# Combining expert rows on GpSimd, one stored copy of the keys, and score maxima sent from SBUF to SBUF, in a Mamba, mixture-of-experts and latent-attention kernel

## The chip, the cores and the metric

The kernel runs on one core of one Trainium2 chip. Times are device microseconds of one execution; a stated time is the median of several runs, and the trace comes from one more execution under the hardware profiler. Five engines share the work: TensorE (PE, with PEld for its weight loads), VectorE (DVE), ScalarE (ACT), GpSimd (POOL) and SyncE (SP, which here only issues DMA transfers and reads indices into registers). POOL and ACT can issue transfers too.

## The reference

The input is x, [4, 512, 128] f32: 4 sequences of 512 tokens. Four residual steps follow one another, each over a layer norm of the whole of x:

```
x = x + A(layernorm(x))      # A: Mamba block, then mixture of experts
x = x + FFN(layernorm(x))    # hidden 384, weights dequantised from int32
x = x + ATT(layernorm(x))    # latent attention, 16 heads of 8, causal
x = x + FFN(layernorm(x))

moe: top_w, sel = top_k(softmax(h @ router_w), 2)
     out = sum over e of (sum of top_w where sel == e) * (silu(h @ Wg[e]) * (h @ Wu[e])) @ Wd[e]

att: c_kv = x @ W_dkv.T                      # 64 wide
     q_lat = (x @ W_dq.T @ W_uq.T) in heads, times k_eff
     a = softmax(causal(q_lat @ c_kv.T / sqrt(8)))
     y = a @ c_kv, per head times v_eff
```

The Mamba block has 256 inner channels, 16 states and a convolution of 4 taps; the mixture has 8 experts of width 512, and each token goes to 2 of them.

## The kernel before

The work has two parts, and the four sequences (b = 0 to 3) move through them like a pipeline.

*First part, to some 378 us.* `scan` (L901) runs 64 steps, one for each sequence and state. A step is a scan on DVE (`hst`, L916), a product on POOL (`hc`, L928), a sum over states on PE (`yp`, L873). Beside the scans four streams of small work are drained in pieces: `closing`, `tokens`, `tiles` and `ends`. When a sequence's 16 steps are done, `close(b)` (L942) makes the Mamba output, adds `base[b] = xs[b] + h2` on POOL (L971), normalises, and calls `route` and `number`, which choose the two experts of each token, their weights `gates[b]` ([128, 4, 2]: token in tile, token tile, rank) and the rows at which the token goes into a sorted array in DRAM. `scatter` (L260) sends the tokens there, `plan(g)` lists for each tile of 128 sorted rows its expert and its place (`cplan`, read by SP into registers at L352 and L353), and `experts(g)` (L333) computes the tiles. `GROUPS = [[0], [1], [2, 3]]`: sequences 0 and 1 are sorted alone, 2 and 3 together. In this part the order on PE, DVE, ACT and SP is the order in which the program is written; POOL's queue is free except that the scan's products are chained in order (`queued`, L881).

*From experts to attention.* For each sequence of a finished group, stream `tokens` runs three generators:

- `combine(b)` (L397): 8 gathers, one for each token tile t and rank k, each issued by POOL as an indirect DMA of 128 rows of 512 B (L413) into one of 8 buffers `yk`; and 8 DVE instructions (L406), `base[:, t] = yk * gate + base[:, t]`. Sequence 0 takes the rows one at a time, the others four at a time, with two turns from gather to use.
- `first_ffn(b)`: `x = base + FFN(layernorm(base))`. The layer norm's statistics are on DVE (`bn_stats` L153, `mv` L155), then `xn` on ACT (L167), transposes on PE (L176), products `pg`, `pu`, `fpd`, and the final addition on POOL (L463).
- `project(b)` (L505): the queries and keys of attention. `pu` (L524) is a matmul for each half (queries, then keys). A value is split into three bf16 parts: the first by ACT (L527), which also copies the whole (`full`, L528), the rest by POOL (L529 to L531). `parts` has one buffer. The queries' parts are stored to `q_d` in DRAM by one DMA (L533); the keys' parts are stored three times to `k_d` (L536), so that a later load finds each part repeated.

*Second part: attention.* It goes by 8 units u, two of each sequence, 8 heads each. In this part a scheduler with a model of the chip sets the order within each engine.

- `fill(u)` (L1122): SP loads two stacks of [128, 8, 512] bf16, `qs` and `ks`, three buffers of each. Rows 0 to 71 of a stack are 3 blocks of 24: each block of `qs` is all three parts of the 8 query dimensions, and block i of `ks` is part i of the keys three times. A single product over the 72 rows is so the sum of all nine products of parts. The last three rows (MXR to P) are -1 in `ks` (L1130) and the row maxima in `qs`.
- `maxima(u)` (L1138): PE makes the masked scores `sc` (L1152, L1156), DVE reduces them to maxima `mx` (L1148), splits them into three bf16 parts (`mparts`), PE transposes these (`pmx`), ACT copies them to `mT` [24, 512] (L1179), and POOL sends `mT` to `m_d` in DRAM (L1181) and from there to the last three rows of `qs` (L1182).
- `exps(G)` (L1188): PE makes the transposed scores minus maxima, `st` (L1205, L1213), ACT the exponentials `p` (L1218). `weigh(G)` sums the values on PE (`po` L1232), transposes, normalises and adds on POOL (`base = x + yn`, L1262).
- `last(b)` runs the final FFN beside later units, and stores the output.

Every tile that `tmp` (L208) makes has as many buffers as its pool, two; the plan's tiles on one partition (`cge`, `cof`, `cat`, `cplan`) are among them.

Of the kernel before, what the change touches and what calls it, by code (L numbers as in the profile page):

```python
# [8 lines left out]
F32 = mybir.dt.float32  # L9
I32 = mybir.dt.int32  # L10
BF16 = mybir.dt.bfloat16
AF = mybir.ActivationFunctionType
ALU = mybir.AluOpType
# [3 lines left out]
P = 128  # L17
B, L, C = 4, 512, 128
NT = L // P
# [6 lines left out]
NH, HS, KVL = 16, 8, 64  # L26
# [11 lines left out]
def block_kernel(ctx, tc, x, rms1_w, rms2_w, in_proj_w, conv_w, conv_b, x_proj_w,  # L38
                 dt_proj_w, dt_proj_b, A_log, D_skip, out_proj_w, router_w, Wg, Wu, Wd,
                 W_dq, W_dqT, W_uqT, W_dkvT, W_uk, W_uv, W_oT, w_gateT, w_upT, w_downT, out):  # L40
    nc = tc.nc
# [143 lines left out]
    base = [keep.tile([P, NT, C], F32, tag="base", name=f"base{b}") for b in range(B)]  # L185
    gates = [keep.tile([P, NT, 2], F32, tag="gates", name=f"gates{b}") for b in range(B)]
    hits = [keep.tile([P, NT, 2, NEXP], F32, tag="hits", name=f"hits{b}") for b in range(B)]
    rows = [keep.tile([P, NT, 2], I32, tag="rows", name=f"rows{b}") for b in range(B)]
    rows_y = [keep.tile([P, NT, 2], I32, tag="rows_y", name=f"rows_y{b}") for b in range(B)]
# [16 lines left out]


    def tmp(name, shape, dt=F32, n=P):  # L208
        return wt.tile([n] + shape, dt, tag=name, name=name)

    taken = {}

# [184 lines left out]
    def combine(b):  # L397

        g = place[b][0]

        n = 4 if b else 1
        which = [(t, k) for t in range(NT) for k in range(2)]
        got = []
        for i in range(0, len(which) + 2 * n, n):
            for yk, t, k in got[max(i - 2 * n, 0) : max(i - n, 0)]:
                nc.vector.scalar_tensor_tensor(  # L406
                    base[b][:, t, :], yk, gates[b][:, t, k : k + 1], base[b][:, t, :],
                    ALU.mult, ALU.add,
                )
            yield  # L410
            for t, k in which[i : i + n]:
                yk = wt.tile([P, C], F32, tag="yk", name="yk", bufs=8)
                nc.gpsimd.indirect_dma_start(  # L413
                    yk, None, sorted_y[g],
                    bass.IndirectOffsetOnAxis(ap=rows_y[b][:, t, k : k + 1], axis=0),
                )
                got.append((yk, t, k))
            yield


# [84 lines left out]
    def project(b):  # L505

        xn = wt.tile([P, NT, C], F32, tag="xn", name="axn", bufs=1)
        yield from layernorm(xn, xs[b])
        xT = wt.tile([P, L], F32, tag="xT", name="axT", bufs=1)
        transposed(ps, xT, xn)  # L510
        yield
        yield
        pq = ps.tile([P, L], F32, tag="mm", name="pq")
        nc.tensor.matmul(pq, w_qk[0], xT, start=True, stop=True)
        qk = wt.tile([P, L], F32, tag="qk", name="qk")
        nc.scalar.copy(qk, pq)
        yield
        q_d = dram0.tile([3, HS, NH, L], BF16, tag="q_d", name="q_d", bufs=2)
        k_d = dram0.tile([3, 3, HS, NH, L], BF16, tag="k_d", name="k_d", bufs=2)
        for half in range(2):  # L520
            yield
            rows = slice(half * KVL, (half + 1) * KVL)
            pq = ps.tile([P, L], F32, tag="mm", name="pu")
            nc.tensor.matmul(pq, w_up[rows, :], qk[rows, :], start=True, stop=True)  # L524
            full = wt.tile([P, L], F32, tag="full", name="full", bufs=1)
            parts = wt.tile([P, 3, L], BF16, tag="parts", name="parts", bufs=1)
            nc.scalar.copy(parts[:, 0, :], pq)  # L527
            nc.scalar.copy(full, pq)  # L528
            nc.gpsimd.tensor_tensor(full, full, parts[:, 0, :], ALU.subtract)  # L529
            nc.gpsimd.tensor_copy(parts[:, 1, :], full)  # L530
            nc.gpsimd.tensor_tensor(parts[:, 2, :], full, parts[:, 1, :], ALU.subtract)  # L531
            if half == 0:
                nc.gpsimd.dma_start(q_d.rearrange("j d h l -> (d h) j l"), parts)  # L533
            else:
                for j in range(3):
                    nc.gpsimd.dma_start(k_d[:, j].rearrange("i d h l -> (d h) i l"), parts)  # L536
            yield
        stores[b] = q_d, k_d, qk

# [543 lines left out]
    with ExitStack() as second:  # L1083
# [18 lines left out]
        NP9, MXR = 9 * HS, P - 3  # L1102
        NU = NH // 2
# [18 lines left out]
        def fill(u):  # L1122

            b, h0 = u // 2, (u % 2) * NU
            q_d, k_d, _ = stores[b]
            if u < 3:
                for h in range(0, NU, 2):
                    for stack in (qs[u], ks[u]):
                        nc.gpsimd.memset(stack[KVL:P, h : h + 2], 0.0)
                nc.sync.dma_start(ks[u][MXR:P], below.unsqueeze(1).to_broadcast([3, NU, L]))  # L1130
            for i in range(3):
                at = slice(3 * HS * i, 3 * HS * (i + 1))
                for stack, of in ((qs[u % 3], q_d), (ks[u % 3], k_d[i])):
                    nc.sync.dma_start(
                        stack[at], of[:, :, h0 : h0 + NU, :].rearrange("j d h l -> (j d) h l")
                    )

        def maxima(u):  # L1138

# [37 lines left out]
                )  # L1177
            mT = w2.tile([3 * NU, L], BF16, tag="mT", name="mT")
            nc.scalar.copy(mT, pm)  # L1179
            m_d = dram.tile([3, NU, L], BF16, tag="m_d", name="m_d")  # L1180
            nc.gpsimd.dma_start(m_d.rearrange("i h l -> (i h) l"), mT)  # L1181
            nc.gpsimd.dma_start(q[MXR:P, :, :], m_d)  # L1182
            yield

        scale = float(HS) ** -0.5
# [208 lines left out]
```

## Time and profile before

| | |
|---|---|
| median of 6 runs | 903.63 us (896.84, 904.18, 902.8, 903.08, 904.52, 905.38) |
| the profiled execution | 909.74 us |
| its span in the trace | 908.0 us |
| its mean granted clock of TensorE | 0.898 |

The page of the profile gives for each engine the time in which it was busy. The same, cut into stretches of the span (busy us of each engine in the stretch):

| stretch, us | what runs | length | PE | DVE | ACT | POOL | DMA share |
|---|---|---|---|---|---|---|---|
| 0 to 378 | scans | 378 | 296.87 | 321.79 | 198.22 | 216.88 | 0.39 |
| 378 to 443 | experts, first projection | 65 | 53.22 | 33.70 | 23.78 | 30.84 | 0.52 |
| 443 to 640 | attention of sequences 0 and 1, experts of 2 and 3 | 197 | 163.34 | 93.96 | 69.14 | 29.17 | 0.54 |
| 640 to 732 | combine and projection of 2, attention of 1 and 2 | 92 | 59.34 | 34.49 | 35.91 | 30.15 | 0.22 |
| 732 to 908 | attention of 2 and 3 | 176 | 140.26 | 86.76 | 84.04 | 22.26 | 0.12 |

The costliest groups of POOL and DVE that lie in the changed lines or beside them, from the group list between 400 and 900 us (line, engine, operation, out<-in, partitions x elements, count | busy us, mean ns of one | idle us of the engine just before them, and what ended it):

```profile
L413 POOL DMA_INDIRECT yk<-yg,rows_y x24 | 23.2, 967 | 84.9 <-DMA yg<-ym 59.0 <-DMA wd<-in_Wd_dram 19.2 <-issue 4.9
...
L536 POOL DMA_DIRECT2D k_d<-parts x12 | 9.3, 774 | 1.2 <-POOL parts L531 1.2
...
L406 DVE SCALAR_TENSOR_TENSOR base<-yk,gates,base 128x128 f32<-128x128 f32 x24 | 8.2, 350 | 6.9 <-DMA yk<-yg,rows_y 6.5 <-issue 0.4
...
L1181 POOL DMA_DIRECT2D m_d<-mT x8 | 4.4, 554 | 63.6 <-ACT mT L1179 63.6
L1182 POOL DMA_DIRECT2D qs<-m_d x8 | 4.2, 529 | 15.2 <-DMA m_d<-mT 8.1 <-PE pg L448 5.5 <-DVE mx L1148 1.7
```

"Idle before" is time in which that engine stood and which ended when the named work did. It costs something only where the engine is one that others wait for. The releaser named is the last one by the profile.

SP's loads of the stacks at L1134 take 0.29 to 0.48 us each to issue (`qs`, median 0.36) and 0.29 to 0.94 (`ks`, median 0.36); the three loads of -1 rows at L1130, whose source is repeated three times, take 0.78 to 0.98.

### The profile page before, as it was taken

The page shows a single profiled execution, that of the slowest core. Times are in us where ns is not written, and L with a number is a line of the kernel's source. Part 1 is how long each engine was busy: PE and PEld are TensorE (multiplying, and loading weights), DVE is VectorE, ACT ScalarE, POOL GpSimd, SP SyncE. Part 2 cuts the span into 40 slices and gives each one's busy share as a digit, 9 for nine tenths or more (in the row PEclk, how much of TensorE's full clock was granted, in tenths as well). Part 3 has the DMA queues.
Part 4 walks back from the last instruction along what each step waited for, and adds up shares of the span by engine and source line. Part 5 has one row for each costly group of instructions (what it writes and reads, how often), then busy time and mean ns, then how long its engine had stood idle before and what let it go on. Part 6 is the DMA issues. An engine that isn't in the chain of part 4 may idle for free.

```text
span 908.0 us, 12207 instructions
## 1 busy us (share of the span) xinstructions
PE 713.0 (79%) x3867; PEld 428.0 (47%) x3867; DVE 570.7 (63%) x1160; ACT 411.1 (45%) x797; POOL 329.3 (36%) x262
## 2 busy tenths in 40 slices
PE   7698697589698975687766998988585698799854
PEld 4433242133276641575554677757242254455432
DVE  4799999989988997554238631336733275457311
ACT  3847556647654540142310354452155353556741
POOL 1155755874774457772213022000613103101010
PEclk9898899889899997899878899999787798799987
DMA  5157211111475644263564166763101502220000
GB/s 133 38 215 271 70 58 50 62 67 58 136 219 181 211 125 126 83 208 125 189 178 126 45 197 216 229 162 120 43 12 38 138 1 57 81 54 15 3 13 12
DMA packets 84481, 99.18 MB, mean 109 GB/s; under 512 B 10369, under 2 KB 56457, under 8 KB 83241
## 3 DMA queue, kind: packets, MB, share of 16 engines
q1 hardware_dynamic: 78881, 87.09, 32.1%
q0 software_dynamic: 4352, 10.89, 3.6%
q8 instruction: 31, 0.51, 0.2%
q10 hardware_dynamic: 1184, 0.43, 0.2%
q14 instruction: 33, 0.27, 0.1%
HBM read 76.67 MB, written 21.63 MB: 108 GB/s over the span
## 4 chain that ended last, share of the span: by engine, by line
PE 35%; DVE 30%; issue 10%; ACT 9%; DMA 7%; POOL 6%; SPq 1%; another core or an unknown queue 0%; DVEq 0%; POOLq 0%; ACTq 0%
DVE hst L916 11%; DVE bx L895 5%; PE yp L873 4%; PE po L1232 4%; DVE mx L1148 3%; PE st L1205 3%; PE mpd L390 3%; POOL hc L928 3%; PE mpg L378 3%; ACT p L1218 3%; PE pg L448 2%; PE mpu L378 2%; PE fpd L457 2%; PE sc L1152 2%; DMA wgu<-in_Wg_dram 1%
## 5 line engine op out<-in xcount | busy, mean ns | idle before, releaser
L928 POOL TENSOR_TENSOR hc<-hst,cs 128x1024 f32<-128x1024 f32 x64 | 152.4, 2382 | 114.8 <-issue 25.8
L873 PE MATMUL yp<-hc,ident 128*128 128x512 f32 x256 | 143.5, 688 | 49.2 <-POOL hc L928 47.1
L916 DVE TENSOR_TENSOR_SCAN hst<-da,bx 128x1024 f32<-128x1024 f32 x64 | 146.3, 2287 | 8.7 <-POOL hc L928 1.3
L1148 DVE TENSOR_REDUCE mx<-sc 128x1 f32<-128x384 f32 (+3 forms) x168 | 102.1, 634 | 54.7 <-PE sc L1156 53.3
L873 PEld LDWEIGHTS yp<-hc,ident 128*128 128x128 f32 x256 | 51.0, 213 | 128.2 <-POOL hc L928 88.0
L1218 ACT ACTIVATE p<-st 128x512 f32<-128x512 f32 x160 | 90.2, 598 | 45.7 <-PE st L1213 24.5
L853 ACT ACTIVATE da<-delta,A 128x512 f32<-128x512 f32 (+1 forms) x128 | 84.9, 714 | 37.1 <-DVE hst L916 30.2
L321 DVE SCALAR_TENSOR_TENSOR thm<-thm,mpg 128x512 f32<-128x512 f32 x53 | 36.1, 681 | 88.4 <-ACT thm L384 88.2
L1152 PE MATMUL sc<-ks,qs 125*128 125x128 bf16 (+3 forms) x256 | 69.2, 324 | 26.9 <-DVE mx L1148 11.2
L895 DVE TENSOR_TENSOR bx<-du,pb 128x1024 f32<-128x1024 f32 x64 | 78.3, 1223 | 4.2 <-PE pb L863 2.0
L1205 PE MATMUL st<-qs,ks 128*128 128x512 bf16 (+3 forms) x256 | 64.1, 318 | 18.4 <-DMA qs<-m_d 7.7
L378 PE MATMUL mpg<-xTm,wgu 128*128 128x128 f32 x424 | 66.2, 293 | 7.3 <-DMA wgu<-in_Wg_dram 4.6
L378 PEld LDWEIGHTS mpg<-xTm,wgu 128*128 128x128 f32 x424 | 58.4, 206 | 19.7 <-issue 8.6
L390 PE MATMUL mpd<-wd,mh 128*128 128x128 f32 x424 | 59.9, 285 | 4.3 <-ACT xTm L371 3.4
L378 PE MATMUL mpu<-xTm,wgu 128*128 128x128 f32 x424 | 60.6, 286 | 2.8 <-DVE mh L322 2.8
L413 POOL DMA_INDIRECT yk<-yg,rows_y x32 | 30.9, 966 | 87.2 <-DMA yg<-ym 59.0
L390 PEld LDWEIGHTS mpd<-wd,mh 128*128 128x128 f32 x424 | 53.0, 196 | 9.5 <-ACT xTm L371 6.6
L378 PEld LDWEIGHTS mpu<-xTm,wgu 128*128 128x128 f32 x424 | 55.9, 203 | 3.3 <-DVE mh L322 3.0
L384 ACT ACTIVATE thm<-mpg 128x512 f32<-128x512 f32 x53 | 31.6, 596 | 54.3 <-PE mpg L378 28.6
L371 ACT ACTIVATE xTm<-mpt,r2w 128x128 f32<-128x128 f32 x53 | 19.4, 365 | 65.7 <-PE mpt L369 65.6
L1156 PE MATMUL sc<-maskq,identb 128*128 128x128 bf16 (+2 forms) x176 | 46.2, 263 | 0.0
L394 ACT COPY ym<-mpd 128x128 f32<-128x128 f32 x53 | 14.1, 265 | 68.8 <-PE mpd L390 49.4
(255 smaller groups left out, 1174.0 us busy)
## 6 DMA issues: line engine op xcount, KB each, us to landing
cs<-c_d SPq DMA_DIRECT2D x64, 256.0 KB
wgu<-in_Wg_dram SPq DMA_DIRECT2D x53, 256.0 KB
wgu<-in_Wu_dram SPq DMA_DIRECT2D x53, 256.0 KB
wd<-in_Wd_dram SPq DMA_DIRECT2D x53, 256.0 KB
xg<-zero SPq DMA_DIRECT2D x8, 1024.0 KB
qs<-q_d SPq DMA_DIRECT2D x24, 192.0 KB
k_d<-parts POOLq DMA_DIRECT2D x12, 384.0 KB
ks<-k_d SPq DMA_DIRECT2D x24, 192.0 KB
```

What stands on the lines that cost most here:

```text
L378: nc.tensor.matmul(pp[:, f, :], w[:, k, f * P : (f + 1) * P], rows_in, start=True, stop=True,)
L390: nc.tensor.matmul(pd, hT[:, f, :], w[:, f, :], start=(f == 0), stop=(f == NFC - 1))
L853: nc.scalar.activation(da[:, e, e:], delta[b][:, e, e:], AF.Exp, scale=A[:, e, n : n + 1])
L873: nc.tensor.matmul(yps[b][:, e, :], ident, hc[:, e, :], start=(n == 0), stop=(n == NS - 1))
L895: nc.vector.tensor_tensor(bxs[s], du[s // NS], taps[s][1].unsqueeze(1).to_broadcast([P, NE, L]), ALU.mult)
L916: nc.vector.tensor_tensor_scan(hst.rearrange("p e l -> p (e l)"), dec.pop(s).rearrange("p e l -> p (e l)"), bxs.pop(s).rearrange("p e l -> ...
L928: done = nc.gpsimd.tensor_tensor(hc, hst, cs.unsqueeze(1).to_broadcast([P, NE, L]), ALU.mult).ins
L1148: nc.vector.tensor_reduce(*taken, AX.X, ALU.max)
L1152: nc.tensor.matmul(sc[:, c : c + w], q[0:MXR, h, t * P : w], k[0:MXR, h, 0:w], start=(h == h0), stop=False, skip_group_check=True,)
L1156: nc.tensor.matmul(sc[:, 0 : n * w].rearrange("p (h k) -> p h k", k=w)[:, :, t * P : w], identb, maskq.unsqueeze(1).to_broadcast([P, n, P] ...
L1205: nc.tensor.matmul(pt[:, c : c + L - kt * P], k[:, h0 + j, rows], q[:, h0 + j, kt * P : L], start=(c == 0), stop=False, skip_group_check=True,
L1218: ready[G] = nc.scalar.activation(p, pt, AF.Exp, scale=scale).ins
```

## The change

Five things change:

1. One-partition tiles of `tmp` get one buffer instead of two.
2. `combine` of sequences 1 to 3: a turn is a token tile, with both its rows gathered into one tile `yk` [128, 2, 128] (two buffers instead of eight of half the size). GpSimd multiplies the tile by the two weights of each token and adds the two halves to `base`, one after the other. Sequence 0 keeps its eight DVE instructions, a row at a time, with the same two buffers.
3. `parts` has two buffers.
4. The keys' parts are stored once, by one DMA like the queries'; a load of a block of `ks` reads the 8 rows of a part three times, through an outer dimension of stride 0.
5. `m_d` is gone. ACT, right behind its copy to `mT`, issues three transfers that each take 8 rows of `mT` to one row of `qs`.

```diff
     def tmp(name, shape, dt=F32, n=P):
-        return wt.tile([n] + shape, dt, tag=name, name=name)
+        return wt.tile([n] + shape, dt, tag=name, name=name, bufs=1 if n == 1 else None)
...
-        n = 4 if b else 1
-        which = [(t, k) for t in range(NT) for k in range(2)]
-        got = []
-        for i in range(0, len(which) + 2 * n, n):
-            for yk, t, k in got[max(i - 2 * n, 0) : max(i - n, 0)]:
-                nc.vector.scalar_tensor_tensor(
-                    base[b][:, t, :], yk, gates[b][:, t, k : k + 1], base[b][:, t, :],
-                    ALU.mult, ALU.add,
-                )
-            yield
-            for t, k in which[i : i + n]:
-                yk = wt.tile([P, C], F32, tag="yk", name="yk", bufs=8)
-                nc.gpsimd.indirect_dma_start(
-                    yk, None, sorted_y[g],
-                    bass.IndirectOffsetOnAxis(ap=rows_y[b][:, t, k : k + 1], axis=0),
-                )
-                got.append((yk, t, k))
-            yield
+        lots = [(t, range(2)) for t in range(NT)] if b else [
+            (t, range(k, k + 1)) for t in range(NT) for k in range(2)
+        ]
+        got = {}
+        for i in range(len(lots) + 2):
+            if i >= 2:
+                yk, t, ks_ = got.pop(i - 2)
+                to = base[b][:, t, :]
+                if b:
+                    nc.gpsimd.tensor_tensor(
+                        yk, yk, gates[b][:, t, :].unsqueeze(2).to_broadcast([P, 2, C]), ALU.mult
+                    )
+                    for k in range(2):
+                        nc.gpsimd.tensor_tensor(to, to, yk[:, k, :], ALU.add)
+                else:
+                    nc.vector.scalar_tensor_tensor(
+                        to, yk[:, 0, :], gates[b][:, t, ks_[0] : ks_[0] + 1], to, ALU.mult, ALU.add
+                    )
+            yield
+            if i < len(lots):
+                t, ks_ = lots[i]
+                yk = wt.tile([P, 2, C], F32, tag="yk", name="yk")
+                for j, k in enumerate(ks_):
+                    nc.gpsimd.indirect_dma_start(
+                        yk[:, j, :], None, sorted_y[g],
+                        bass.IndirectOffsetOnAxis(ap=rows_y[b][:, t, k : k + 1], axis=0),
+                    )
+                got[i] = yk, t, ks_
+            yield
...
-        k_d = dram0.tile([3, 3, HS, NH, L], BF16, tag="k_d", name="k_d", bufs=2)
+        k_d = dram0.tile([3, HS, NH, L], BF16, tag="k_d", name="k_d", bufs=2)
...
-            parts = wt.tile([P, 3, L], BF16, tag="parts", name="parts", bufs=1)
+            parts = wt.tile([P, 3, L], BF16, tag="parts", name="parts", bufs=2)
...
-            if half == 0:
-                nc.gpsimd.dma_start(q_d.rearrange("j d h l -> (d h) j l"), parts)
-            else:
-                for j in range(3):
-                    nc.gpsimd.dma_start(k_d[:, j].rearrange("i d h l -> (d h) i l"), parts)
+            nc.gpsimd.dma_start((q_d, k_d)[half].rearrange("j d h l -> (d h) j l"), parts)
...
-                for stack, of in ((qs[u % 3], q_d), (ks[u % 3], k_d[i])):
-                    nc.sync.dma_start(
-                        stack[at], of[:, :, h0 : h0 + NU, :].rearrange("j d h l -> (j d) h l")
-                    )
+                nc.sync.dma_start(
+                    qs[u % 3][at], q_d[:, :, h0 : h0 + NU, :].rearrange("j d h l -> (j d) h l")
+                )
+                nc.sync.dma_start(
+                    ks[u % 3][at],
+                    k_d[i, :, h0 : h0 + NU, :].unsqueeze(0).to_broadcast([3, HS, NU, L]),
+                )
...
-            m_d = dram.tile([3, NU, L], BF16, tag="m_d", name="m_d")
-            nc.gpsimd.dma_start(m_d.rearrange("i h l -> (i h) l"), mT)
-            nc.gpsimd.dma_start(q[MXR:P, :, :], m_d)
+            for i in range(3):
+                nc.scalar.dma_start(q[MXR + i : MXR + i + 1, :, :], mT[NU * i : NU * (i + 1), :])
```

Seen from the queues: POOL loses 16 issues for the maxima and 8 key stores, and gains 12 multiplications and 24 additions; DVE loses 24 instructions; ACT gains 24 issues. In the order of the changed kernel, the last two gathers of sequence 0 stand behind the sum `base` of sequence 3 (L971) on POOL, and one gather instead of three stands ahead of the last scan product.

## The prediction

> **What bounds the kernel now.** I read the busy shares first, then the costly groups and the list of waits of the second part (440 to 910 us), then stretches and single instructions where a named wait is long. The second part is where most of the changed lines run.
>
> ```profile
> PE 713.0 (79%) x3867; PEld 428.0 (47%) x3867; DVE 570.7 (63%) x1160; ACT 411.1 (45%) x797; POOL 329.3 (36%) x262
> ```
>
> PE leads with 79%, but it is not full everywhere. Stretches of 20 us (columns: stretch, length, busy us of PE, PEld, DVE, ACT, POOL with instruction counts, granted clock, DMA share, GB/s) show where it starves:
>
> ```profile
> 640.00:660.00 20.00, 8.94 (x37) 4.13 (x37) 14.04 (x47) 0.81 (x3) 14.94 (x17) 0.67 0.16 45
> 700.00:720.00 20.00, 10.93 (x28) 5.19 (x29) 5.55 (x8) 6.72 (x13) 6.30 (x8) 0.71 0.63 160
> 760.00:780.00 20.00, 13.68 (x64) 7.72 (x64) 14.76 (x43) 4.54 (x8) 11.12 (x13) 0.74 0.51 144
> ```
>
> Between 500 and 640 the same view sums to 126.9 us of PE in 140: there PE itself is the bound. The list of waits from 440 on (engine and line, what it waited for: us in total, times, longest) names what starves it:
>
> ```profile
> ACT parts L527 <- DMA q_d<-parts: 17.3, 4, 6.6
> ...
> POOL qs L1182 <- DMA m_d<-mT: 8.1, 4, 2.8
> ...
> PE st L1205 <- DMA qs<-m_d: 7.7, 2, 5.1
> ...
> PE sc L1152 <- DVE mv L155: 7.2, 1, 7.2
> ...
> DVE base L406 <- DMA yk<-yg,rows_y: 6.5, 9, 1.7
> ...
> PE sc L1152 <- DMA ks<-k_d: 5.2, 1, 5.2
> ```
>
> Each of these is touched by the change. The chain that ended last runs through the key store and the key load before the first scores:
>
> ```profile
> 457.85 5.73 DMA k_d<-parts
> ...
> 464.46 4.73 DMA ks<-k_d
> ```
>
> On POOL three spots matter: three gathers ahead of the last scan product, the projection's second half, and the row of gathers of sequence 2 with the q row's two transfers among them.
>
> ```profile
> 362.97 0.94 POOL L413 DMA_INDIRECT yk<-yg,rows_y  x1 [0.30 <-issue]
> 363.93 2.36 POOL L928 TENSOR_TENSOR hc<-hst,cs 128x1024 f32<-128x1024 f32 x1
> ...
> 452.95 1.14 POOL L529 TENSOR_TENSOR full<-full,parts 128x512 f32<-128x512 f32 x1 [4.99 <-ACT full L528]
> ...
> 456.30 2.32 POOL L536 DMA_DIRECT2D k_d<-parts  x3 [0.30 <-POOL parts L531]
> ...
> 640.80 1.04 POOL L413 DMA_INDIRECT yk<-yg,rows_y  x1 [58.97 <-DMA yg<-ym]
> ...
> 713.42 0.52 POOL L1182 DMA_DIRECT2D qs<-m_d  x1 [5.47 <-PE pg L448]
> ```
>
> **The change, part by part.** The sum is made against the profiled execution (909.7 us, span 908.0), 6 us above the median of 903.63; I subtract its result from the median.
>
> *Scans' end.* The last product waited behind three gathers, from 360.4 to 363.9, though its scan ended at 358.2; in the changed order one gather stands there. Two gathers less at 0.96 + 0.30 us: -2.5. The last two gathers of sequence 0 now come behind base(3) (L971), and their two vector instructions (0.35 us each, plus some 2.5 us from issue to landing) stand ahead of the rms of sequence 3 on DVE: bounds 0 to +2, taken +0.5. Together **-2**.
>
> *Start of attention, 443 to 490.* With two parts buffers the second half need not wait for the q store (4.94 us in the chain, 3.16 us of ACT, 4.99 us of POOL): -5.0. The key store is one issue instead of three. Three stores landed 7.3 us after 456.3, while q's single store took 4.6 (447.1 to 451.7): -2.7. The loads could start about 7.7 us earlier. Two things give back. Key loads that repeat rows have no row of their own; the nearest issue rows are plain ones at 0.36 us and one repeated three times (L1130) at 0.83, so three per unit cost 0 to +1.5 in issue, and with longer landing I bound it at 0 to +3, taken +1.5. And combine 1 moves onto POOL: 8 gathers of 1.26 (10.1 us) as before, plus four turns. POOL's product takes 1.26 us for 128x512 and 2.38 for 128x1024, so 0.14 + 2.2 ns an element: 0.70 for the weighting (128x256) and 2 x 0.42 for the additions, with gaps 1.7 a turn, 6.8 in all. Sequence 1's base was ready at 493.0, on DVE; on POOL I get about 477.8 + 10.1 + 6.8 = 494.7 less what the earlier start gives: +1.7. Sum **-4.5**. The 24 vector instructions that vanish (8.2 us busy) are not counted: DVE is idle half the time here, and its statistics of base still stand between the reductions and now wait for POOL's additions.
>
> *500 to 640.* PE can gain at most its 13.1 idle us. Here lies sequence 1's projection, with a parts wait of 2.3 (545.45). I take **-3** (0 to -6).
>
> *640 to 732.* Removed: the stall of PE's scores at 651.95 (7.2, behind DVE's statistics, themselves behind the gathers), the parts wait at 700.57 (6.6), and the q row's path: mT copied by 704.7, both transfers through DRAM, st not before 721.91 (5.1 idle). Added: combine 2. In the changed order its last turn comes after 10 gathers, 3 turns earlier: 640.8 + 12.6 + 6.8 = 660.2 against 652.6 before, so +7.6; and sequence 2's normalised rows are transposed on PE after only 2 score blocks instead of 9 or 10, so PE stands for them. Of the 18.9 removed, some 9 are lost to PE idling for xn, and most of the rest to the same delay: **-2** (bounds -12 to +6).
>
> *732 to the end.* The parts wait at 766.35 (5.2) lies in a stretch where PE idles 6.3 of 20; the q rows' detour ends for three more units: **-5** (0 to -8).
>
> *q rows from ACT.* 24 transfers leave POOL's queue (16 issues of 0.54 us, 8.6 us) and go to ACT's, three a unit. Direct issues cost 0.29 to 0.98 us elsewhere, so 7 to 24 us of ACT, behind which p (0.6 us each, what PE's next products wait for), parts and axn queue. ACT is 45% busy, so mostly hidden; one per unit at 0.36 on the path: **+3**. Behind that stands a coupling: in the changed order these issues also wait on completion semaphores which SP's loads use, and SP's loads on theirs. No row before shows it; bounds 0 and 3 us a unit (a part of the 4.7 us that a load took to land), taken 0.25: **+2**.
>
> One buffer for one-partition tiles is costed at nothing: the plan of the last group may be written only when SP has read that of the group before. In the changed order SP's last such read stands just ahead of the load that began at 417.4 (L1130), and the write behind DVE's third th, which began at 419.7: some 2 us to spare. If SP were later, DVE's fh behind the write, and PE's fpd behind that, would wait as long.
>
> Sum: -2 - 4.5 - 3 - 2 - 5 + 3 + 2 = **-11.5**, so 903.6 - 11.5 = **892 us**.
>
> A page speaks against the key loads. The row first: in a stretch of loads the DMA share is 0.74 at 164 GB/s, and in a full one 1.02 at 396.
>
> ```profile
> 70.00:77.00 7.00, 6.50 (x16) 2.43 (x15) 6.74 (x7) 6.96 (x10) 2.45 (x2) 1.00 1.02 396
> 713.00:715.00 2.00, 1.45 (x4) 0.54 (x4) 0.84 (x3) 0.60 (x1) 0.52 (x1) 1.00 0.74 164
> ```
>
> The Trainium skill, "DMA: Bandwidth & Descriptors", section "Why a DMA increments its semaphore by 16 and not by 1", says that a transfer uses the largest number of engines up to 16 that divides the slowest dimension, other than one, of both sides. For 24 rows on both sides that is 12 of 16 or 0.75, as the row shows; for 3 repeats of 8 rows it would be 3, which no run here shows yet. An estimate from page and rows: 3/16 of 396 is some 74 GB/s, so 196.6 KB would take 2.7 us instead of 1.2, +4.5 us a unit; if all eight were exposed the sum would be +23 and not -11.5.
>
> **The rivals.** *B, all waits pay.* The list above that is removed sums to 17.3 + 7.2 + 7.7 + 5.2 = 37.4, with the scans' end 39; if combine hides behind PE's experts, two thirds arrive: -26, **878**. For it: PE's idle stretches coincide with them. Against: 500 to 640, where PE is full, and the 7.6 us by which combine 2 is later.
>
> *C, nothing comes of it.* If the projections were hidden anyway (the -3 and -5 vanish) and combine 2 costs 2 more, -11.5 + 8 + 2 = -1.5, **902**. For it: the units' order is written by a model, and units have up to three stacks filled ahead. Against: the idle of 640 to 780.
>
> *D, slower.* The coupling of ACT and SP. At each unit ACT stands at its q-row issues until an older load of SP has landed; p, parts and axn queue behind it, PE waits for p. At 3 us a unit it is 8 x 3 = 24 on top of 892: **916**. It decides from 11.5 / 8 = 1.4 us more a unit than I took. For it: 24 issues, and loads that take 4.7 us to land. Against: loads are mostly issued a unit ahead.
>
> **How the numbers follow.** The forecast has 0.45 with an own range of 884 to 899 (the ends of its terms offsetting each other in part), B 0.12, C 0.20, D 0.23. Half a per cent, 4.5 us, is what a measurement of this kernel can tell. Faster than 899.1: all of the forecast but 0.01 and B, 0.56. Within: C without its upper edge, and that 0.01, 0.20. Slower than 908.1: D and C's edge, 0.24. For 8 in 10 the range runs from 877, where it leaves out half of B, to 914, where it leaves out some half of D.
>
> **What would show it.** Right: parts (L527) without a wait for q_d's store; ks loads starting near 456; no scores waiting for DVE's mv; st not waiting for the q row. Rule of the page: DMA share near 0.19 in a stretch of key loads alone. Wrong: ACT idle ahead of its q-row issues with SP's loads as releaser (D); PE idle at transposes for xn of sequences 2 and 3 by more than 10 us (towards C); the stretches of 640 and 700 as empty as before.

## The result and the profile after

The change makes the kernel slower: 912.21 us (median of 20 runs, 908.22 to 916.46) against 904.38 us of the kernel before (46 runs beside them), ratio 1.0099 with a 95% interval of 1.008 to 1.0118. The forecast was 892, faster.

The profiled execution has a span of 909.3 us, 1.3 above the profiled one of before, which was itself 5 us above its median; so the two traces show where time moved, and the runs how much. Busy us of PE, PEld, DVE, ACT and POOL by stage of the changed kernel (columns as in the prediction):

```profile
443.00:640.00 197.00, 158.94 (x1153) 120.87 (x1152) 92.62 (x191) 68.13 (x150) 30.11 (x37) 0.90 0.50 151
640.00:732.00 92.00, 64.76 (x363) 33.97 (x363) 35.89 (x131) 39.63 (x77) 39.01 (x51) 0.81 0.17 49
732.00:909.00 177.00, 134.48 (x940) 74.21 (x938) 81.69 (x224) 80.88 (x153) 16.27 (x15) 0.90 0.08 24
```

Against the table of before, PE did 4.4 us less between 443 and 640, 5.4 more between 640 and 732, and 5.8 less in the last stage although that is a microsecond longer. The list of waits from 440 on names the new ones (the lines have moved by up to 12; L1163 is the scores, L153 the statistics of `base`, L415 the additions of `combine`):

```profile
PE sc L1163 <- DMA ks<-k_d: 19.4, 3, 14.4
...
DVE st L153 <- POOL base L415: 17.2, 7, 3.2
...
ACT xTm L371 <- DMA qs<-mT: 4.2, 1, 4.2
```

The 17.3 us in which `parts` waited for the store of `q_d` are gone, as meant: no line of the list has that wait. In their place the scores wait 19.4 us for keys where they waited 5.2, DVE waits 17.2 us for POOL's additions, and ACT waits behind its own transfers of the maxima (the last line and three others, 12.4 us in all). The chain that ended last shows the keys at the start of attention (440 to 500):

```profile
452.45 4.57 DMA k_d<-parts
457.05 0.78 SPq L1144
...
461.59 17.36 DMA ks<-k_d
478.98 4.51 DMA xt<-xg
...
483.79 1.03 POOL yk L425
```

The store of the keys landed at 457.0 and not at 463.6, 6.6 us earlier. Yet the first scores start 2.1 us later. From PE's timeline, first before the change and then after:

```profile
469.32 0.58 PE L1152 MATMUL sc<-ks,qs 125*128 125x128 bf16 x4 [5.17 <-DMA ks<-k_d]
```

```profile
471.40 0.59 PE L1163 MATMUL sc<-ks,qs 125*128 125x128 bf16 x4 [14.45 <-DMA ks<-k_d]
```

And a key load of unit 1, issued at 461.6 and landed 17.4 us later, held up SP's later transfers, the experts' tokens (`xt`) among them, so that sequence 1's gathers began at 483.8 instead of 477.8. In the trace the transfers of SP and ACT go round eight completion semaphores: the `xt` transfer of 478.98 uses the semaphore of that key load and waits for it. SP's own list of waits from 440 on has six such lines, 31.4 us behind key loads in all where the kernel before had 7.8; the longest:

```profile
SPq L1144 <- DMA ks<-k_d: 8.7, 3, 4.3
```

### The profile page after: what moved, and what is told of

Its sections match the earlier page's. It is cut to its first block, busy times and chain, and to the rows that moved or that the text cites. A ratio compares the mean times of both kernels' runs of the same rounds, so it can differ in the third digit from the quotient of the medians.

```text
span 909.3 us, 12178 instructions
## 1 busy us (share of the span) xinstructions
PE 711.2 (78%) x3867; PEld 428.4 (47%) x3867; DVE 562.7 (62%) x1136; ACT 410.3 (45%) x797; POOL 332.2 (37%) x274
## 4 chain that ended last, share of the span: by engine, by line
PE 35%; DVE 25%; DMA 11%; ACT 9%; POOL 9%; issue 7%; SPq 2%; another core or an unknown queue 1%; ACTq 0%; POOLq 0%; DVEq 0%
DVE hst L924 9%; DMA ks<-k_d 4%; PE yp L881 4%; DVE bx L903 4%; PE po L1242 4%; POOL hc L936 3%; PE mpg L378 3%; PE mpu L378 3%; ACT p L1228 3%; PE mpd L390 2%; PE pg L460 2%; PE st L1215 2%; PE fpd L469 2%; PE sc L1163 2%; POOL yk L425 2%
## 5 line engine op out<-in xcount | busy, mean ns | idle before, releaser
L1163 PE MATMUL sc<-ks,qs 125*128 125x128 bf16 (+3 forms) x256 | 66.4, 315 | 42.0 <-DMA ks<-k_d 19.4
L378 PEld LDWEIGHTS mpg<-xTm,wgu 128*128 128x128 f32 x424 | 59.4, 209 | 23.0 <-issue 10.6
L371 ACT ACTIVATE xTm<-mpt,r2w 128x128 f32<-128x128 f32 x53 | 19.4, 366 | 61.5 <-PE mpt L369 56.9
```

The source lines that it names most:

```text
L378: nc.tensor.matmul(pp[:, f, :], w[:, k, f * P : (f + 1) * P], rows_in, start=True, stop=True,)
L1163: nc.tensor.matmul(sc[:, c : c + w], q[0:MXR, h, t * P : w], k[0:MXR, h, 0:w], start=(h == h0), stop=False, skip_group_check=True,)
```

## The experiments

Ratios are to the kernel before, run beside each version; its median lay between 896 and 904 us from one set of runs to the next, so that ratios are compared and not microseconds. 0.001 is 0.9 us; a single ratio is known to some 0.004, a difference of two to some 0.005. No version leaves out part of the computation.

### The keys' loads: rows in another order, or three stores

Version 1 keeps everything but the order of the 24 rows in a block of both stacks, so that the three copies of a row are adjacent. PE, DVE, ACT and POOL run the same instructions in the same order as in the changed kernel. The queries' rows, which repeat nothing, change their order too.

```diff
-                    qs[u % 3][at], q_d[:, :, h0 : h0 + NU, :].rearrange("j d h l -> (j d) h l")
+                    qs[u % 3][at], q_d[:, :, h0 : h0 + NU, :].rearrange("j d h l -> d j h l")
...
-                    k_d[i, :, h0 : h0 + NU, :].unsqueeze(0).to_broadcast([3, HS, NU, L]),
+                    k_d[i, :, h0 : h0 + NU, :].unsqueeze(1).to_broadcast([HS, 3, NU, L]),
```

> The changed kernel with one difference: the 24 rows of a block of both stacks lie dimension by dimension (each of the 8 rows of a key part three times in a row) instead of part by part, so that the repeated source has an outer dimension of 8 and no longer of 3. The order of the instructions on PE, DVE, ACT and POOL is the same as in the changed kernel. Theory 1, the repeated key loads are slow because only a few DMA engines carry them: in the changed kernel six key loads from 457.1 on let the first scores start at 471.4 (14.45 us of PE idle), and 3.0, 2.5 and 11.2 us stand at later units. With loads at about the rate of before (4.7 us to land) the first scores start near 463, -8 there, and some -6 at units 6 and 7: 912 - 12 = about 900 us, ratio to before 0.995; in stretches with only key loads the DMA share no longer lies flat at 0.18 to 0.20. The Trainium skill's rule (DMA: Bandwidth & Descriptors, Why a DMA increments its semaphore by 16 and not by 1) would make it 8 engines of 16, a share of 0.5. Theory 2, the combine on GpSimd is the cost (sequence 1's and 2's base come 5.1 and 14 us later than before): within 3 us of 912. Theory 3, the transfers that ACT issues are the cost (12.4 us of ACT waits behind them): within 3 us of 912.

Measured: 891.09 us, 0.9857 (0.9817 to 0.9897).

Version 2 stores the keys three times and loads plain rows, as before the change; parts, maxima and combine stay changed. The cut leaves out the stores and the load, which are those of the kernel before.

```diff
-        k_d = dram0.tile([3, HS, NH, L], BF16, tag="k_d", name="k_d", bufs=2)
+        k_d = dram0.tile([3, 3, HS, NH, L], BF16, tag="k_d", name="k_d", bufs=2)
...
```

> The changed kernel with the keys' part undone: three stores into a k_d of nine slabs, plain loads of 24 rows. Theory 1: the loads take 0.36 us to issue and about 4.7 to land as before, the store takes 7.3 instead of 4.6: -12 + 2.7 at the start and some 2 at the units of sequences 2 and 3, about 904 us, ratio 1.00, a little slower than the version with rows in the other order. Theories 2 and 3: within 4 us of 912, or slower, since POOL has two more issues for each sequence.

Measured: 893.08 us, 0.9876 (0.9838 to 0.9914).

Theory 1 holds in its direction, and the effect is larger than it said: the way the rows are loaded is worth 0.024 of the time, 21 us. Since PE has the same 3867 instructions in the same order in the changed kernel and in version 1, the distance of the two traces can be followed from place to place: under 1 us to 457, 4.6 us at the first scores (471.4 and 466.8), 9.0 at the first `st` (526.5 and 517.5), 11.1 at 594.0, 13.3 at 727.4 in the scores of unit 4, and 20.4 at 794.9 behind those of unit 6; it is 20.0 at 896. So less than half arises at the start. The load of unit 1 that took 17.4 us took 6.8 in version 1, and SP stood 7.7 us behind key loads instead of 31.4.

Stretches of 2 us in which hardly anything but stack loads ran (last columns: granted clock, DMA share, GB/s) show why the loads were slow; first the changed kernel, then version 1, then version 2:

```profile
466.00:468.00 2.00, 0.00 (x0) 0.00 (x0) 0.00 (x0) 0.00 (x0) 0.00 (x0) 0.50 0.23 74
468.00:470.00 2.00, 0.00 (x0) 0.00 (x0) 0.00 (x0) 0.00 (x0) 0.00 (x0) 0.50 0.19 78
```

```profile
462.00:464.00 2.00, 0.00 (x0) 0.00 (x0) 0.00 (x0) 0.00 (x0) 0.00 (x0) 0.50 0.48 115
464.00:466.00 2.00, 0.00 (x0) 0.00 (x0) 0.00 (x0) 0.00 (x0) 0.00 (x0) 0.50 0.54 188
```

```profile
460.00:462.00 2.00, 0.00 (x0) 0.00 (x0) 0.00 (x0) 0.00 (x0) 0.00 (x0) 0.50 0.78 164
462.00:464.00 2.00, 0.67 (x5) 0.56 (x6) 0.00 (x0) 0.00 (x0) 0.00 (x0) 0.50 0.77 168
```

The shares are near 3/16, 8/16 and 12/16. That fits the rule of the Trainium skill (DMA: Bandwidth & Descriptors, Why a DMA increments its semaphore by 16 and not by 1): as many engines as the largest number up to 16 that divides the slowest dimension of both sides, 3 repeats and 24 rows, 8 rows and 24, 24 and 24. With 3 the rate agrees as well: 74 to 78 GB/s where the prediction's estimate from page and rows was 74. With more it does not go up in step with the share, 115 and 188 at 8, 164 and 168 at 12, so the estimate by share alone is no rule.

The new form costs issue time too, by the source view of the loads (ns, least, median, most): a key load takes 0.70 us with the repeat outermost and 0.64 with it inside, against a median of 0.36 for plain rows before. It is not the repeat: the queries' loads of version 1, which repeat nothing but have their 24 rows in two dimensions, take 0.64 as well.

```profile
L1144 SPq DMA_DIRECT2D ks<-k_d x24: 676/696/775, 457.0 to 789.0; - x24
```

### Combine on DVE, and the maxima through DRAM

Version 3 is the changed kernel with the weighting on DVE:

```diff
-                    nc.gpsimd.tensor_tensor(
-                        yk, yk, gates[b][:, t, :].unsqueeze(2).to_broadcast([P, 2, C]), ALU.mult
-                    )
-                    for k in range(2):
-                        nc.gpsimd.tensor_tensor(to, to, yk[:, k, :], ALU.add)
+                    for k in ks_:
+                        nc.vector.scalar_tensor_tensor(
+                            to, yk[:, k, :], gates[b][:, t, k : k + 1], to, ALU.mult, ALU.add
+                        )
```

> The changed kernel with one difference: the rows of sequences 1 to 3 are weighted and added by DVE, two instructions of 0.35 us a token tile, from the same two buffers and in the same turns. Theory 2: POOL's turn of 0.62 + 2 x 0.45 us and the gathers that queue behind it fall away, 4 x 1.7 = 6.8 us for each of three sequences, two of them exposed: -10, about 902 us. Theory 1: the gathers keep waiting for their two buffers, the bound stays the key loads: within 4 us of 912. Theory 3: the same as theory 1.

Measured: 905.13 us, 1.0015 (0.9991 to 1.0038), so 0.008 below the change: theory 2 has a part, though not the whole.

Version 4 is the changed kernel with `m_d` and POOL's two transfers back:

```diff
-            for i in range(3):
-                nc.scalar.dma_start(q[MXR + i : MXR + i + 1, :, :], mT[NU * i : NU * (i + 1), :])
+            m_d = dram.tile([3, NU, L], BF16, tag="m_d", name="m_d")
+            nc.gpsimd.dma_start(m_d.rearrange("i h l -> (i h) l"), mT)
+            nc.gpsimd.dma_start(q[MXR:P, :, :], m_d)
```

> The changed kernel with one difference: the maxima's rows go by POOL through DRAM again, two transfers in series. Theory 3: ACT no longer issues 24 transfers of 0.63 us (15 us) and the waits of xTm, p, th and va behind them (12.4 us) fall away, some 8 of them on the path: about 904 us. Theory 1: the q row was worth 5 to 8 us in units whose st waited for it (7.7 us before), and those come back: 912 to 919 us. Theory 2: POOL's queue is the tighter one, so slower by more than 8 us: over 920.

Measured: 897.65 us, 0.9925 (0.9895 to 0.9954), 0.017 below the change. Each of these edits alone takes 7 to 21 us off; the effects overlap. Version 4 also has another order of instructions on PE.

### The same two edits beside faster key loads

> The version with the rows in the other order (891.1 us), and the maxima's rows by POOL through DRAM as before. With the slow key loads this same step took 14.6 us off the changed kernel. Theory A, what ACT's transfers cost is their own: 3 issues of 0.63 to 1.2 us stand between ACT's instructions of each unit (waits of th, p and xTm behind them: 12 us), whatever the key loads do: -8 to -14, about 880 us. Theory B, they cost through the key loads: transfers of SP and ACT complete on the same eight semaphores, so slow key loads hold up the next transfers of both queues (at 779.6 to 789.0 us SP's last four loads of keys stood 9 us apart in all, without ACT's transfers 774.3 to 777.1); with faster loads the step is worth nothing or loses the q row's path: 889 to 899 us.

Measured (version 5, version 1 with version 4's edit): 886.90 us, 0.9828 (0.9794 to 0.9861). Beside the faster loads ACT's three transfers cost 0.003, within what can be told. So theory B, or something like it: most of what they cost comes with the slow keys.

> The version with the rows in the other order (891.1 us), with the weighting and adding of sequences 1 to 3 on DVE. With slow key loads the same step took 7 us off. If POOL's 6.8 us a sequence are exposed by themselves (sequence 2's x was ready 4 to 8 us later on POOL than it could be): -4 to -8, about 885 us. If only the slow keys had made that gap: 889 to 893 us.

Measured (version 6, version 1 with version 3's edit): 880.67 us, 0.9755 (0.9714 to 0.9796), 0.010 below version 1. The combine on POOL costs some 9 us by itself. POOL's timeline of the changed kernel shows a turn:

```profile
647.17 0.63 POOL L411 TENSOR_TENSOR yk<-yk,gates 128x256 f32<-128x256 f32 x1
647.87 0.98 POOL L415 TENSOR_TENSOR base<-base,yk 128x128 f32<-128x128 f32 x2
649.13 1.00 POOL L425 DMA_INDIRECT yk<-yg,rows_y  x1 [0.27 <-POOL base L415]
650.43 0.95 POOL L425 DMA_INDIRECT yk<-yg,rows_y  x1 [0.30 <-issue]
```

A turn is 0.63 + 0.98 us, and the next gathers queue behind it. Sequence 2's last addition ends at 661.5 where its last DVE instruction ended near 652.6 before. In the meantime PE starves: up to 666.5 it waits 10.6 us for sequence 2's normalised rows (`xn`), where before it had no such wait, but stood 7.2 us for `mv`. The stretch 650 to 670, first before the change and then after:

```profile
650.00:670.00 20.00, 14.39 (x48) 6.16 (x47) 10.98 (x43) 8.09 (x16) 9.51 (x11) 0.57 0.12 35
```

```profile
650.00:670.00 20.00, 6.40 (x23) 2.75 (x22) 7.40 (x27) 4.01 (x9) 16.52 (x25) 0.50 0.12 33
```

### What parts and the turns of combine are worth

Version 7 is the change with the keys and the maxima as before it and the weighting on DVE. What stays is `parts` with two buffers and what makes room for it: one buffer for one-partition tiles, and `combine` in six turns with two `yk` tiles.

> Two buffers for parts, and what made room for them (one buffer for one-partition tiles, two yk tiles with six turns), with the combine on DVE, the keys stored three times, the maxima through DRAM: of the change only the waits of parts L527 and of the projection's second half are gone. By the prediction's steps: -2 at the scans' end, -5 + 0.5 at the start, -3, and -5 of sequences 2 and 3's parts waits: 904 - 12 = 892 us. If the parts waits were hidden anyway: 900 to 904 us.

Measured: 881.30 us, 0.9755 (0.9724 to 0.9787).

The next version is version 7 with one buffer for `parts`:

```diff
-            parts = wt.tile([P, 3, L], BF16, tag="parts", name="parts", bufs=2)
+            parts = wt.tile([P, 3, L], BF16, tag="parts", name="parts", bufs=1)
```

> The version with parts alone (881.3 us), with parts back at one buffer: what stays of the change is one buffer for one-partition tiles and the six turns of combine with two yk tiles, on DVE. If the 22 us of that version are the waits for the store of q_d (17.3 us of L527, 4.9 us of POOL in the chain): back to 898 to 904 us. If they come from the turns of combine (the stall of scores behind DVE's mv, 7.2 us, and the gathers ahead of the last scan product): 884 to 892 us. Both share it if it ends at about 893.

Measured: 881.46 us beside a kernel before that stood at 897.87: 0.9825 (0.9789 to 0.9861). So the six turns and their room bring 0.0175, 16 us; no run parts the turns from the room. The second buffer for parts brings 0.007, 6 us, a difference between two sets of runs whose intervals just miss each other, so anything from nothing to 12 us. The traces put the gain of the turns down to the order: with two gathers a turn in place of four, the scheduler lets the experts' tiles run beside the first maxima (80 of their products `mpg`, `mpu` and `mpd` in 40 us, 32 before). The 40 us from the first scores on, before the change and then in this version:

```profile
469.00:509.00 40.00, 30.14 (x145) 17.18 (x146) 32.18 (x79) 4.06 (x9) 7.74 (x8) 0.78 0.40 111
```

```profile
460.00:500.00 40.00, 34.63 (x191) 22.18 (x191) 34.37 (x82) 6.25 (x14) 7.75 (x8) 0.75 0.56 162
```

PE does 4.5 us more in them, and from the first scores to the copy of unit 0's maxima (`mT`) it is 44.2 us here and 52.0 before. The next gain lies around sequence 2's combine: from `mT` of unit 2 to that of unit 3 it is 53 us for 64.5, and no scores wait for DVE's `mv`, which cost 7.2. These two traces are 30 us apart, where the medians are 16: they show places, not sizes.

### One transfer by ACT for all three rows

```diff
-            for i in range(3):
-                nc.scalar.dma_start(q[MXR + i : MXR + i + 1, :, :], mT[NU * i : NU * (i + 1), :])
+            nc.scalar.dma_start(q[MXR:P, :, :], mT)
```

> The version with the rows in the other order (891.1 us), with one transfer by ACT of all 24 rows of mT to the three rows of qs in place of three. Theory A: two issues of 0.63 us less in each of 8 units, 10 us of ACT, 3 to 6 on the path: 885 to 888 us. Theory B: within 2 us of 891, but for what another order of instructions brings, since this edit moves instructions on PE.

Measured (version 1 with this edit): 874.78 us, 0.9671 (0.9640 to 0.9703), 0.019 below three transfers: more than either theory gave.

> The rows in the other order, the combine on DVE, and one transfer by ACT for the maxima. Against three transfers (880.7 us): if the 16 us that one transfer brought beside the combine on POOL are the time of two issues in each unit, the same here, 865 to 870 us; if they came from the order in which that version's instructions happened to be placed on PE, anything from 872 to 884 us.

Measured: 866.15 us, 0.9652 (0.9611 to 0.9694), 0.010 below the version with three (version 6).

> The version with parts alone (881.3 us: keys stored three times, combine on DVE), with one transfer by ACT for the maxima in place of two by POOL through DRAM. If the q row's path is worth what it showed before the change (7.7 us of st waiting, 8.1 us of POOL): 870 to 876 us. If it is hidden: 879 to 883 us. Against the version with rows in the other order it also shows whether one store and loads that repeat rows are worth anything: the same within 3 us if not.

Measured: 865.08 us, 0.9642 (0.9605 to 0.9679), 0.011 below version 7. These two are the fastest of all, 3.5 and 3.6% below the kernel before and some 4.5% below the change. Between them storing the keys once and repeating rows at the load is worth nothing that can be told against three stores. One transfer also gives PE another order than three, so its gain is not shown to be the issues that it saves.

### Why slow keys and ACT's transfers cost more together

> The version with parts alone (881.3 us), with the keys as in the change: one store, and loads that repeat 8 rows three times with the repeat outermost. PE has the same order. If the loads on three DMA engines are the cost by themselves: the first scores 8 us later and the units of sequences 2 and 3 another 6 to 10, 896 to 902 us. If they only cost together with ACT's transfers (semaphores shared by the queues): 883 to 889 us.

Measured (version 7 with the keys as in the change): 878.44 us, 0.9779 (0.9743 to 0.9815), only 0.002 above version 7, from another set of runs. That left a corner to explain: with the combine on DVE, slow keys cost 0.002 without ACT's transfers and 0.026 with three. Four runs varied the number of transfers; those with the rows in the other order have their slow partner's order of instructions on PE, DVE, ACT and POOL.

> Key loads as in the change (repeat outermost), combine on DVE, one transfer by ACT for the maxima. Its partner with the rows in the other order has the same order of instructions on every compute engine and stood at 0.9652 of before; what the slow key loads cost is the difference to it: 0.0024 without transfers of ACT, 0.0260 with three a unit. If each transfer of ACT collides with the slow loads: a third, 0.973 of before. If the cost depends on where the order puts the scores behind the loads: anything from 0.967 to 0.99.

Measured: 879.65 us, 0.9817 (0.9776 to 0.9858), 0.017 above its partner where a third of what three cost would be 0.009.

> Key loads as in the change, combine on DVE, the three transfers of the maxima issued by SP in place of ACT (with them by ACT: 1.0015 of before). If it is ACT's standing at its issues (2.0 to 4.2 us a unit) that costs beside slow loads: 0.98 to 0.985. If it is that the transfers themselves wait for the loads, or the loads for them: 1.00 to 1.01, or more, since in SP's queue they stand right behind the loads.

Measured: 888.56 us, 0.9908 (0.9872 to 0.9944): the same three transfers by SP are 0.011 to 0.012 cheaper than by ACT, less than if ACT's standing were all, more than if only the transfers' own waits counted.

> Key loads as in the change, combine on DVE, and ACT's three transfers of a unit cut into six of half the size. Twice the issues: if each transfer of ACT costs beside slow loads, 1.015 to 1.025 of before; if three or six are alike and the cost was the order that three happened to bring: 0.98 to 1.005.

Measured: 886.96 us, 0.9911 (0.9880 to 0.9942): six cost less than three.

> The same six transfers, with the rows in the other order (three: 0.9755 of before). If ACT's transfers cost nothing beside fast loads: 0.973 to 0.979. If each costs by itself some 0.003, as between one transfer (0.9652) and three: 0.985 to 0.995. Against the run with slow loads the difference is what the loads cost at six transfers: over 0.03 by the collision, 0.002 to 0.02 by the order.

Measured: 873.65 us, 0.9752 (0.9715 to 0.9790), the same as with three.

Since the ends of this comparison came from different sets of runs, the two were run again side by side.

> The version with the change's keys alone again (0.9779 of before), beside the next kernel in the same call. The two were measured in different calls, in which the kernel before stood at 897.87 and 903.69 us: the same kernel may lose more to slow loads in one than in the other. If the corner of the table is real: again 0.974 to 0.982.

Measured: 887.30 us, 0.9832 (0.9801 to 0.9864).

> The change with the combine on DVE again (1.0015 of before). If the corner of the table is real: 0.998 to 1.005, 20 us or more above the other kernel of this call. If it came from the call: 0.985 to 0.995, and the difference that three transfers of ACT make beside slow loads is 8 to 15 us and no longer 21.

Measured: 905.42 us, 1.0032 (1.0001 to 1.0064). The corner stays, somewhat smaller than expected: 18 us between the two. The table:

| combine on | transfers by ACT a unit | keys' rows in the other order, or stored three times (first line) | key loads as in the change | difference |
|---|---|---|---|---|
| DVE | none | 0.9755 | 0.9779, again 0.9832 | 0.002 to 0.008 |
| DVE | 1 | 0.9652 | 0.9817 | 0.017 |
| DVE | 3 | 0.9755 | 1.0015, again 1.0032 | 0.026 to 0.028 |
| DVE | 6 | 0.9752 | 0.9911 | 0.016 |
| POOL | none | 0.9828 | 0.9925 | 0.010 |
| POOL | 3 | 0.9857 | 1.0099 | 0.024 |

It isn't the number of transfers, so the theory that each collides with slow loads falls. PE's waits for transfers in these last two kernels (from 440 on), first without ACT's transfers, then with three:

```profile
PE sc L1162 <- DMA ks<-k_d: 14.3, 1, 14.3
PE st L1215 <- DMA qs<-m_d: 3.9, 1, 3.9
```

```profile
PE sc L1162 <- DMA ks<-k_d: 16.2, 3, 10.7
PE st L1214 <- DMA qs<-mT: 5.2, 1, 5.2
PE mpt L369 <- DMA xt<-xg: 3.8, 1, 3.8
```

Without them the keys are waited for once, at the start; with three also at two later units (5.5 us), and the experts' tokens come late behind them in SP's queue. In the second kernel ACT also stood 8.6 us for stores of expert rows that SP issues. What each form of the transfer changes besides itself is the order that the scheduler gives PE and SP: some 480 of PE's 3860 instructions stand in another place with three than with none. SP's queue stands about as long behind key loads in both, 32.5 us without and 35.7 with three. The likeliest reading is that the order decides how soon after a key load its scores, or the experts' tokens behind it, are due; but no run changed the order alone, and it stays open.

## Why the prediction was wrong

**The step that failed.** It is the key loads in the part on the start of attention: "three per unit cost 0 to +1.5 in issue, and with longer landing I bound it at 0 to +3, taken +1.5", charged once for a single place. Undone with no instruction of PE, DVE, ACT or POOL moved (version 1), these loads were worth 21 us. From the end of the key store to the first scores the changed kernel took 14.4 us (457.0 to 471.4) where the one before took 5.7 (463.6 to 469.3) and version 1 7.8, so +8.7 at that place alone; and the loads of units 6 and 7, issued from 777.6 on, went out until 789.0 and held the scores at 790.8. Two things went wrong in the term. Its size came from rows for issue, and it had no row for the landing of a repeated source. And it looked only at the scores that wait for the keys, where SP's other transfers stood 31.4 us behind slow key loads and delayed the experts' tokens and the loads of later units. The page that spoke against the change had a price: its +4.5 a unit, and +23 in place of -11.5 if all were exposed, is somewhat nearer to the measured +7.8 (0.0099) than the forecast is. It was stated and then given no weight.

**Without it** the sum comes out, but not for its reasons. The prediction without its 1.5 for the loads is 890.6; versions 1 and 2, with everything else of the change, took 891.1 and 893.1. That agreement is largely luck, because the terms were sized wrongly in both directions:

- *Scans' end, -2.* The last product started at 361.0 and not 363.9, as forecast, though two traces of one later version differ by 2.5 us there (357.8 and 360.3).
- *Parts.* The waits went as said: the second half of the projection at 447.9 instead of 451.8, the key store landed 6.6 us earlier for 7.7 forecast. But of the -13 that I credited to the three stages in which they stand, the runs show some -6 for the second buffer, known to no better than 0 to -12: the later waits seem to have been mostly hidden.
- *Turns of combine.* With the combine on DVE they and their room brought -16, where I had only the scans' end and a part of 640 to 732. I priced the waits that the new order removes and not what PE would do in them.
- *Combine on POOL.* Sequence 2 took 19.2 us from its first gather to its last addition, for 19.4 forecast, and sequence 1 18.3 for 16.9; the runs put its price at 7 to 13 us, near the 1.7 and most of 7.6 that went into the sum. One of the signs of being wrong that I had named came true here: PE stood 10.6 us at the transposes for sequence 2's `xn`; with the combine on DVE it stood 6.4 there (version 6) or not at all (version 3).
- *ACT's transfers, +3 and +2.* Beside loads with a higher DMA share three of them cost 0 to 0.003 against two transfers through DRAM. They take 1.96 to 4.10 us of ACT a unit, and the 12.4 us of waits behind them are then mostly hidden.

**The rivals.** The result lies near where D put it (916), and slow loads and ACT's transfers do cost more together. But D's mechanism, ACT standing at its issues until a load has landed, isn't what the runs show: from first issue to last ACT's transfers took 18.9 us in all eight units of the changed kernel and 18.1 in version 1, 0.8 us more where D had 24. Six transfers also cost less than three, and three from SP still cost 0.991. So D was near by luck. C's condition, later projections that were hidden anyway, seems half true, but it too had no term for the slow loads. B's 878 is about what the change's good parts bring (881, and 865 with one transfer and the combine on DVE), though B had it from the parts' waits above all, and the larger part came with the turns.

## What to carry to other kernels

Where a load repeats its source, ask how many DMA engines it can use before asking what it costs to issue, and put the repeat inside a longer dimension: here the same bytes in another row order were worth 2.4% in the changed kernel, and 0.2 to 2.8% in its variants. Ask also what stands behind a slow load in its queue, here 31.4 us of SP's other transfers. When the only price of a new form stands on a page and no row bounds it from above, the range must reach to that price. And edits that move transfers between queues didn't add up here, where each brings another order; so run a change's parts alone and in pairs before keeping the whole.

## What was not expected of the hardware

DMA share went with the outer dimension of the load: 0.19 to 0.23 at 3, 0.48 to 0.54 at 8, 0.77 to 0.78 at 24. One DMA by ACT from 24 rows of SBUF to 3 served as well as three, with 9 to 19 us less in the whole. A load whose rows lie in two dimensions takes 0.64 to 0.70 us to issue from SP, with or without a repeat, plain rows 0.36. The medians of the kernel before, 896 to 904 us from one set of runs to the next, lie about as far apart as the change moved it.
